# Attention's query products as three one-pass products of split operands, with keys and values for two batch elements at a time

## The chip, the cores and the metric

The kernel runs on one core of a Trainium2 chip. A core has a matrix engine (PE, whose weight loads are shown as PEld), a vector engine (DVE), a scalar engine (ACT), a general engine (POOL, also called GpSimd) and a queue for transfers (SP). Each engine takes its instructions in order and waits where an operand isn't there. PE writes its sums to PSUM, which has eight banks of 128 x 512 floats[...]. The metric is the time of one execution on the device, in microseconds, lower is better.

## The reference

The input x has 16 batch elements of 512 rows and 512 columns, the context 16 elements of 120 rows. The layer is cross attention with 16 heads of 32 columns and then a feed-forward layer with quantized weights and activations. In short:

```
xn   = layernorm(x)
q, k, v = xn @ Wq, ctx @ Wk, ctx @ Wv
q, k = rope(q), rope(k)
x1   = x + softmax(q k^T / sqrt(32)) v @ Wo
h    = act_qdq(layernorm(x1))        # scale: max |h| over all of x1
gate, up = act_qdq(h @ Wg^T), act_qdq(h @ Wu^T)
out  = x1 + act_qdq(act_qdq(gate * sigmoid_q(gate)) * up) @ Wd^T
```

`act_qdq` rounds to 16 bit with one scale for the whole tensor, so its scale is a maximum over everything before it. The weights of the feed-forward layer are rounded to 4 bit in blocks of 32.

## The kernel before

The kernel has three stages: attention (up to about 943 us), gate and up products, and the down product. Only attention and its hand-over are touched by the change.

In attention the loop `for b in range(B)` goes over the 16 elements, with a loop over four groups `g` of four heads inside. One iteration works on several elements at once: `here` (b) has its scores, exponentials and values computed; `nxt` (b + 1) has its queries projected and rotated; `new` (b + 2) is loaded, has row statistics, is normalized and turned so that its columns lie on partitions; `old` (b - 1) has its values divided by the sums, multiplied by Wo and added to x; `older` (b - 2) has its rows of x1 normalized and the maximum of |h| taken (`end_normalize`, `largest`). Beside this the keys and values of later elements are made by `Keys`, four elements at a time (`BC = 4`), in twelve parts that `go_on` hands out two or so per group, and in each of elements 1 to 12 a block of gate weights is quantized and split (`WeightBlock`).

The order on PE, DVE and ACT is the order in which the program is written (`manual_schedule`). POOL and the transfer queue are ordered by the planner of the framework. PSUM is divided into three single banks that everything takes in turn (`bank`, tag "w"), two pairs for the scores and one for the sums. So an operation that takes a bank waits until the third taker before it has been read.

Within a group the order is: `scores` (matmuls L338, then DVE takes maxima over rows, L344), some product of another element that fills PE, `maxima` (PE transposes the maxima, `tm`, L356, and DVE makes their negative, `nm`, L365), `values` of the group before, `exponentials` (PE subtracts the maxima, L373, ACT takes the exponential, L381). After that come the rest of the group's parts, such as outputs of `old` and, in group 3, the turning of `new`, the output of the last row block, and the turning of the gate weight.

The queries are exact float products: `query(g)` multiplies four blocks of 128 rows of the turned x (`xnT`, two buffers) with Wq (L317), and `rotate` applies the rotary tables with DVE and POOL. In the feed-forward stage the same accuracy is had otherwise: an operand is split into a high and a low part (`Pieces`: mix, lo, hi), and three products in a one-pass format are added, with one division of the bank by ACT between the first and the other two (`sums`, `MIXED`, `WHOLE`).

Of the kernel before, what the change touches and what calls it, by code (L numbers as in the profile page):

```python
# [21 lines left out]
P = 128  # L22
# [20 lines left out]
HI_BITS = -4096  # L43
TO_256 = 1.5 * 2.0 ** 31
# [9 lines left out]
def tile_xattn_ffn(  # L54
# [24 lines left out]
    BC = 4  # L79
# [14 lines left out]
    max_x = const.tile([P, B * NQ], F32, name="max_x")  # L94
# [93 lines left out]
    with ExitStack() as at:  # L188
# [18 lines left out]
        def transposed(src, rows, dst, nm):  # L207

            n = src.shape[1] // P
            tp = bank(f"tp_{nm}").rearrange("p (n r) -> p n r", r=P)  # L210
            for i in range(n):
                nc.tensor.transpose(tp[:, i, :rows], src[:, ts(i, P)], ident[:rows, :rows])
            nc.scalar.copy(dst, tp[:, :n, :rows])  # L213
# [18 lines left out]
        class Keys:  # L232


            def __init__(self, c):
# [5 lines left out]
                if c == 0:  # L241
# [4 lines left out]
                self.parts = [  # L246
                    (f, i) for f in (self.context, self.value, self.key) for i in range(BC)
                ]

            def go_on(self, n):  # L250
                for _ in range(n):
                    if self.parts:
                        f, i = self.parts.pop(0)
                        f(i)

            def context(self, i):
                if self.c == 0:
                    ct = self.ct[:, i, :]
                else:
                    ct = p1.tile([SK, D], F32, tag="ct", name=f"ct_{self.c}_{i}")  # L260
                    nc.sync.dma_start(ct, cx[self.c * BC + i])
                transposed(ct, SK, self.cT[:, :, ts(i, SK)], f"c_{self.c}_{i}")

            def value(self, i):
                ps = bank(f"vp_{self.c}_{i}")
# [5 lines left out]
                nc.scalar.copy(self.vt[:, i, :], ps[:SK])  # L271

            def key(self, g):
                ps = bank(f"kp_{self.c}_{g}")[:, :SKC]
# [6 lines left out]
                rotate(self.kT[:, g, :, :SK], ps, bc(cos_k), bc(sin_k), f"k_{self.c}_{g}")  # L281
                nc.gpsimd.tensor_copy(self.kT[:, g, :, SK:], self.kT[:, g, :, : P - SK])

        class Element:


            def __init__(self, b):
                self.b = b
                self.xt = p2.tile([P, NQ, D], F32, tag="xt", name=f"xt_{b}", bufs=4)
                nc.sync.dma_start(self.xt, x[b].rearrange("(q p) d -> p q d", p=P))  # L290
                self.mv = p2.tile([P, NQ, 2], F32, tag="mv", name=f"mv_{b}")
                self.rstd = p2.tile([P, NQ], F32, tag="rstd", name=f"rstd_{b}")
                self.xnT = p1.tile([P, ND, S], F32, tag="xnT", name=f"xnT_{b}")
                self.qs, self.xn = [], {}
# [6 lines left out]
            def normalize(self, q, engine=nc.gpsimd):  # L301
                xn = p2.tile([P, D], F32, tag="xn", name=f"xn_{self.b}_{q}", bufs=3)
# [6 lines left out]
            def turn(self, q):  # L309
                transposed(self.xn.pop(q), P, self.xnT[:, :, ts(q, P)], f"x_{self.b}_{q}")  # L310

            def query(self, g):

                nm = f"{self.b}_{g}"
                ps = bank(f"qp_{nm}")
                for d in range(ND):
                    nc.tensor.matmul(  # L317
                        ps, lhsT=wq_sb[:, d, ts(g, P)], rhs=self.xnT[:, d, :],
                        start=(d == 0), stop=(d == ND - 1),
                    )  # L320
                def rest():
                    qT = p1.tile([P, S], F32, tag="qT", name=f"qT_{nm}", bufs=5)
                    rotate(qT, ps, cos_q, sin_q, f"q_{nm}")
# [96 lines left out]
            def output(self, q):  # L420

                ps = bank(f"op_{self.b}_{q}")
# [5 lines left out]
                def rest():  # L428
                    b, x1 = self.b, self.xt[:, q, :]
                    nc.vector.tensor_tensor(x1, ps, x1, ALU.add)  # L430
                    row_stats(p2, x1, ln_mv[:, b, q, :], f"f_{b}_{q}")
                return rest
# [9 lines left out]

            def end_normalize(self, q, engine=nc.gpsimd):
                b = self.b
# [1089 lines left out]
```

## Time and profile before

Three runs took 2604.33 us in the median (2603.31 to 2606.76). The profiled execution took 2608.83 us, with a span of 2607.0 us.

| stage | us | PE busy | DVE busy | ACT busy | POOL busy | clock |
|---|---|---|---|---|---|---|
| start, 0 to 58 | 58 | 51.85 | 26.18 | 9.90 | 22.90 | 1.00 |
| elements 0 to 14, 58 to 862 | 804 | 776.27 | 633.14 | 210.25 | 487.14 | 0.99 |
| element 15, 862 to 911 | 49 | 39.17 | 31.96 | 12.68 | 10.31 | 0.90 |
| end of attention, 911 to 943 | 32 | 25.57 | 22.66 | 1.34 | 17.33 | 0.87 |
| feed-forward, 943 to 2607 | 1664 | 1619.80 | 1369.62 | 921.69 | 1038.97 | 0.99 |

"Busy" is the time in which the engine had an instruction under way. The clock is the share of full speed that TensorE was granted. The table says which engine is full in a stage; what a wait is worth has to be read from the timeline, since engines run in order and a wait of one delays all that stands behind it. In a timeline line the first number is the start in us from the span's start, the second the length; then engine, line, operation, the tile written and those read, the shape and how many instructions were merged. A note in brackets gives the idle time before it and what ended it.

### The profile page before, as it was taken

The page shows a single profiled execution, that of the slowest core. Times are in us where ns is not written, and L with a number is a line of the kernel's source. Part 1 is how long each engine was busy: PE and PEld are TensorE (multiplying, and loading weights), DVE is VectorE, ACT ScalarE, POOL GpSimd, SP SyncE. Part 2 cuts the span into 40 slices and gives each one's busy share as a digit, 9 for nine tenths or more (in the row PEclk, how much of TensorE's full clock was granted, in tenths as well). Part 3 has the DMA queues.
Part 4 walks back from the last instruction along what each step waited for, and adds up shares of the span by engine and source line. Part 5 has one row for each costly group of instructions (what it writes and reads, how often), then busy time and mean ns, then how long its engine had stood idle before and what let it go on. Part 6 is the DMA issues. An engine that isn't in the chain of part 4 may idle for free. (4 is left out here: it accounts for less than half of the span.)

```text
span 2607.0 us, 30411 instructions
## 1 busy us (share of the span) xinstructions
PE 2512.7 (96%) x10732; PEld 1690.9 (65%) x10732; DVE 2083.6 (80%) x2836; ACT 1155.9 (44%) x1311; POOL 1576.6 (60%) x1011
## 2 busy tenths in 40 slices
PE   8899999999999889999999999999999699999999
PEld 4334344333433268888878888888887478788887
DVE  4668886887888667786887589999998688888886
ACT  1222232222222225545445378888877344444442
POOL 3466665655675165545555057777766477777775
PEclk9899999999999989999999999999999799999999
DMA  4011121111120086767766789999889777777774
GB/s 161 20 65 49 49 93 59 57 59 49 49 77 33 22 277 214 250 202 244 226 217 217 238 300 332 322 344 330 296 290 322 295 280 253 248 248 248 251 249 145
DMA packets 268146, 500.49 MB, mean 192 GB/s; under 512 B 47440, under 2 KB 66000, under 8 KB 267984
## 3 DMA queue, kind: packets, MB, share of 16 engines
q1 hardware_dynamic: 267296, 496.90, 55.6%
q8 instruction: 85, 1.39, 0.2%
q10 hardware_dynamic: 528, 1.05, 0.1%
q14 instruction: 77, 0.63, 0.1%
q0 software_dynamic: 160, 0.52, 0.1%
HBM read 263.00 MB, written 227.54 MB: 188 GB/s over the span
## 5 line engine op out<-in xcount | busy, mean ns | idle before, releaser
L758 POOL TENSOR_SCALAR oh_d<-oq_d 128x512 fp32r<-128x512 int16 x190 | 398.0, 2117 | 160.8 <-DVE oq_d L1320 134.1
L1106 POOL TENSOR_TENSOR po<-gt,t_wu 128x1024 f32<-128x1024 f32 x96 | 231.7, 2413 | 208.2 <-DVE gt L1083 149.6
L317 PE MATMUL qp<-xnT,wq_sb 128*128 128x512 f32 x512 | 239.2, 610 | 2.5 <-ACT cT L213 2.5
L398 ACT COPY ao<-pv 128x512 f32<-128x512 f32 x64 | 37.5, 586 | 452.2 <-PE pv L389 452.2
L424 PE MATMUL op<-wo_sb,ao 128*128 128x512 f32 x512 | 233.2, 604 | 0.2 <-DVE ao L418 0.2
L1337 PE MATMUL dn_d<-wd,om_d 128*128 128x512 f32 x768 | 196.7, 406 | 22.7 <-DVE om_d L768 13.4
L782 PE MATMUL mm_wg<-xl_g,wg 128*128 128x512 f32 x768 | 205.4, 389 | 0.0
L782 PE MATMUL mm_wg<-xh_g,wg 128*128 128x512 f32 x768 | 205.4, 389 | 0.0
L868 PE MATMUL mm_wg<-xm_g,wg 128*128 128x512 f32 x768 | 195.7, 396 | 6.8 <-DVE xm_g L768 3.6
L1320 DVE SCALAR_TENSOR_TENSOR oq_d<-pq_d,r_o,uq_d 128x1024 int16<-128x1024 int16 x96 | 127.3, 1326 | 90.1 <-ACT uq_d L1273 90.1
L229 POOL TENSOR_TENSOR rt_q<-rt_q,sin_q 128x512 f32<-128x512 f32 x64 | 81.3, 1271 | 185.0 <-DVE rt_q L226 185.0
L1337 PEld LDWEIGHTS dn_d<-wd,om_d 128*128 128x128 f32 x768 | 145.9, 194 | 68.3 <-DVE om_d L768 31.0
L758 POOL TENSOR_SCALAR xh_g<-xq_g 128x512 fp32r<-128x512 int16 x60 | 117.5, 1982 | 116.6 <-DMA xq_g<-xi 111.2
L1337 PE MATMUL dn_d<-wd,ol_d 128*128 128x512 f32 x768 | 184.6, 389 | 1.0 <-ACT dn_d L1349 1.0
L1337 PE MATMUL dn_d<-wd,oh_d 128*128 128x512 f32 x768 | 184.5, 389 | 0.0
L782 PE MATMUL mm_wu<-xl_u,wu 128*128 128x512 f32 x672 | 180.5, 390 | 1.3 <-ACT mm_wu L874 1.3
L317 PEld LDWEIGHTS qp<-xnT,wq_sb 128*128 128x128 f32 x512 | 93.3, 192 | 134.9 <-issue 111.0
L782 PE MATMUL mm_wu<-xh_u,wu 128*128 128x512 f32 x672 | 179.7, 389 | 0.0
L344 DVE TRANSPOSE_TENSOR_REDUCE mt<-st 128x32 f32<-128x1024 f32 x128 | 151.6, 1222 | 30.2 <-PE st L338 30.1
L891 DVE TENSOR_REDUCE max_g<-t_wg 128x1 f32<-128x1024 f32 x96 | 116.5, 1214 | 72.4 <-ACT t_wg L886 72.4
L424 PEld LDWEIGHTS op<-wo_sb,ao 128*128 128x128 f32 x512 | 94.5, 192 | 116.9 <-issue 104.6
L868 PEld LDWEIGHTS mm_wg<-xm_g,wg 128*128 128x128 f32 x768 | 142.9, 190 | 38.9 <-DVE xm_g L768 6.3
(266 smaller groups left out, 5682.7 us busy)
## 6 DMA issues: line engine op xcount, KB each, us to landing
g_d<-t_wg SPq DMA_DIRECT2D x96, 512.0 KB, 3.7
gt<-g_d SPq DMA_DIRECT2D x96, 512.0 KB, 5.4
u_d<-t_wu SPq DMA_DIRECT2D x90, 512.0 KB, 5.8
p_d<-gt SPq DMA_DIRECT2D x90, 512.0 KB, 5.1
p<-p_d SPq DMA_DIRECT2D x90, 512.0 KB, 6.0
u<-u_d SPq DMA_DIRECT2D x90, 512.0 KB, 5.3
xt<-in_x_dram SPq DMA_DIRECT2D x16, 1024.0 KB, 5.3
x_d<-x SPq DMA_DIRECT2D x32, 512.0 KB, 5.0
```

Source lines behind the costliest of these rows:

```text
L229: nc.gpsimd.tensor_tensor(v(t), v(t), sin, ALU.mult)
L317: nc.tensor.matmul(ps, lhsT=wq_sb[:, d, ts(g, P)], rhs=self.xnT[:, d, :], start=(d == 0), stop=(d == ND - 1),)
L344: nc.vector.tensor_reduce(self.mt[:, 2 * i : 2 * i + 2, 0, :], self.st[i].rearrange("p h (c j) -> p h c j", j=DK), AX.X, ALU.max, apply_tr ...
L398: nc.scalar.copy(self.ao[:, g, :], pv)
L424: nc.tensor.matmul(ps, lhsT=self.ao[:, g, ts(q, P)], rhs=wo_sb[:, g, :], start=(g == 0), stop=(g == NG - 1),)
L758: engine.tensor_scalar(as_runs(p.hi, q), q, TO_256, TO_256, ALU.add, ALU.subtract)
L782: nc.tensor.matmul(ps[:, j, :], lhsT=lhs(j, i)[k], rhs=rhs(j, i)[k], start=(k == 0 and i == 0), stop=(k != 1 and i == n - 1), skip_group_c ...
L868: nc.tensor.matmul(self.ps[:, j, :], lhsT=lhs(j, d), rhs=self.x.p[d].mix, start=(d == 0), stop=(d == ND - 1), skip_group_check=True,)
L891: nc.vector.tensor_reduce(maxes[:, i : i + 1], self.t, AX.XYZ, ALU.max, **how)
L1106: nc.gpsimd.tensor_tensor(flat(g.po), flat(g.tile), flat(c.t), ALU.mult)
L1320: nc.vector.scalar_tensor_tensor(out=oq.rearrange("p f t -> p (f t)"), in0=pq, scalar=r_o, in1=uq, op0=ALU.mult, op1=ALU.mult,)
L1337: nc.tensor.matmul(self.ps[j], lhsT=self.p[f // 2].all()[k][:, f % 2, ts(j, P)], rhs=wd.made[f][k], start=(k == 0 and f == 0), stop=(k != ...
```

## The change

- **Queries.** The turned block of x is no longer kept as one exact tile. `turn(q)` writes it back over the normalized rows and masks its high bits (DVE) to `up`, of which there are two buffers. `halve(q)` copies these to `hi` (ACT) and subtracts them from the full value for `lo` (POOL). `mixed(q)` multiplies `lo` by -4096 (ACT) and adds `hi` for `mix` (POOL). The three pieces have one buffer each. Wq is split in the same way before the loop (`query_weight`).
- **Query sums.** `query(g)` makes the first four one-pass products (mix) and ACT divides the bank; `query_rest(g)` makes the other eight (lo, hi) and returns the rotation. Eight instructions become twelve. The factor that makes up for the division goes into the rotary tables.
- **Keys and values.** `BC` is 2; there are eight batches with eight parts each, four parts per element, and key products have 240 columns instead of 480.
- **x1.** The rows of x are loaded again for the output (`load("xr")`), with three buffers instead of four. The sum `x1` is made by an instruction that also gives each row's maximum, and DVE takes the row's minimum. `end_normalize` and `largest` go; at the end the maxima and minima are normalized (two operations on 128 x 128 values), and the largest magnitude is taken from them.
- **Order.** Fillers between `scores` and `maxima` are put in two lists: `soon` runs before `maxima`, `late` after it. The first passes of queries 0 and 1 come after the exponentials of group 0 where keys are made.

The diff, cut to its core:

```diff
-    BC = 4
+    BC = 2
...
-                self.xt = p2.tile([P, NQ, D], F32, tag="xt", name=f"xt_{b}", bufs=4)
-                nc.sync.dma_start(self.xt, x[b].rearrange("(q p) d -> p q d", p=P))
+                self.load("xt")
...
+            def load(self, nm):
+                self.xt = p2.tile([P, NQ, D], F32, tag="xt", name=f"{nm}_{self.b}", bufs=3)
+                nc.sync.dma_start(self.xt, x[self.b].rearrange("(q p) d -> p q d", p=P))
...
             def turn(self, q):
-                transposed(self.xn.pop(q), P, self.xnT[:, :, ts(q, P)], f"x_{self.b}_{q}")
+                if q == 0:
+                    self.mix, self.lo, self.hi = self.pieces = [
+                        p1.tile([P, ND, S], F32R, tag=f"xn{k}", name=f"xn{k}_{self.b}", bufs=1)
+                        for k in "mlh"
+                    ]
+                full = self.xn[q].rearrange("p (d r) -> p d r", r=P)
+                transposed(self.xn[q], P, full, bank(f"tp_{self.b}_{q}"))()
+                self.up[q] = p2.tile([P, ND, P], F32, tag="xu", name=f"xu_{self.b}_{q}")
+                nc.vector.tensor_scalar(
+                    self.up[q].bitcast(I32), full.bitcast(I32), HI_BITS, None, ALU.bitwise_and
+                )
+
+            def halve(self, q):
+                m, l, h = (t[:, :, ts(q, P)] for t in self.pieces)
+                full = self.xn.pop(q).rearrange("p (d r) -> p d r", r=P)
+                nc.scalar.copy(h, self.up[q])
+                nc.gpsimd.tensor_tensor(l, full, h.bitcast(F32), ALU.subtract)
+
+            def mixed(self, q):
+                m, l, h = (t[:, :, ts(q, P)] for t in self.pieces)
+                low = self.up.pop(q)
+                nc.scalar.mul(low, l.bitcast(F32), -SPLIT)
+                nc.gpsimd.tensor_tensor(m, low, h.bitcast(F32), ALU.add)
+
+            def query_sums(self, g, ks):
+                for k in ks:
+                    for d in range(ND):
+                        nc.tensor.matmul(
+                            self.qp[g], lhsT=wq_pieces[k][:, d, ts(g, P)],
+                            rhs=self.pieces[k][:, d, :], start=(k == 0 and d == 0),
+                            stop=(k != 1 and d == ND - 1), skip_group_check=True,
+                        )
 
             def query(self, g):
...
+                self.qp[g] = bank(f"qp_{self.b}_{g}")
+                self.query_sums(g, (0,))
+                nc.scalar.mul(self.qp[g], self.qp[g], MIXED)
+
+            def query_rest(self, g):
+                self.query_sums(g, (1, 2))
                 def rest():
...
-                    nc.vector.tensor_tensor(x1, ps, x1, ALU.add)
+                def add():
+                    nc.vector.tensor_tensor_reduce(
+                        out=x1, in0=ps, in1=x1, scale=1.0, scalar=-LARGEST, op0=ALU.add,
+                        op1=ALU.max, accum_out=ends_x[:, b, q, 0:1],
+                    )
+                def stats():
                     row_stats(p2, x1, ln_mv[:, b, q, :], f"f_{b}_{q}")
+                    nc.vector.tensor_reduce(ends_x[:, b, q, 1:2], x1, AX.X, ALU.min)
+                return add, stats
...
+            if old:
+                old.load("xr")
+            if nxt:
+                nxt.halve(NQ - 1)
+                nxt.mixed(NQ - 2)
+                nxt.mixed(NQ - 1)
+            here.attend()
             for g in range(NG):
+                here.scores(g, keys[b // BC].kT)
+                soon, late = [], []
                 if g == 0:
+                    if kvs:
+                        kvs.go_on()()
+                        late.append(kvs.go_on())
+                    elif nxt:
+                        nxt.query(0)
+                        nxt.query(1)
+                        late.append(nxt.query_rest(0))
+                if g == 1:
+                    first_bank = bank("kv") if kvs else None
+                    if nxt:
+                        nxt.query(2)
+                    if kvs:
+                        soon.append(kvs.go_on(first_bank))
+                    if nxt:
+                        late.append(nxt.query_rest(2))
+                if g == 2:
+                    first_bank = bank("op") if old else None
+                    if nxt:
+                        nxt.query(3)
+                    if old:
+                        add, stats = old.output(0, first_bank)
+                        soon.append(add)
+                        late.append(stats)
+                    if nxt:
+                        late.append(nxt.query_rest(3))
+                if g == 3 and old:
+                    late += old.output(2)
+                for f in soon:
+                    f()
                 here.maxima(g)
...
                 if g == 0:
+                    if nxt and kvs:
+                        nxt.query(0)
+                        nxt.query(1)
                     if old:
                         old.reciprocals()
+                    if nxt and kvs:
+                        nxt.query_rest(0)()
                     if nxt:
-                        nxt.query(1)()
+                        nxt.query_rest(1)()
...
                 if g == 3:
                     if new:
                         new.turn(0)
-                        new.normalize(3)
                     if old:
-                        old.output(3)()
+                        for f in old.output(3):
+                            f()
                         old.end()
                         old.inverse()
                     if new:
                         new.turn(1)
+                        new.halve(0)
                     if weight:
                         rest = weight.turn(0)
                     if new:
+                        new.mixed(0)
                         new.turn(2)
+                        new.halve(1)
+                        new.mixed(1)
                         new.turn(3)
+                        new.halve(2)
                     if weight:
                         rest()
```

## The prediction

> **What bounds the kernel now.** I read the page's engine table and 40 slices first. The attention stage is the left third: there PE is 9 or 8 in nearly every slice while DVE is at 4 to 8. The chain of waits that ended last holds only lines of the feed-forward stage, so it says nothing about this change. I therefore cut the attention stage into its elements. Element b begins with its first score matmuls (L338): b = 4 at 277.9 us, b = 6 at 377.1, b = 7 at 438.1. Columns are length, then busy time of PE, PEld, DVE, ACT, POOL, then clock.
>
> ```profile
> 277.90:326.50 48.60, 47.10 (x205) 18.70 (x204) 43.69 (x79) 13.46 (x19) 31.99 (x30) 1.00 0.20 65
> ...
> 377.10:438.10 61.00, 60.33 (x237) 24.48 (x236) 43.04 (x79) 15.85 (x23) 32.02 (x30) 1.00 0.15 53
> 438.10:498.40 60.30, 59.63 (x237) 24.71 (x236) 47.72 (x91) 13.48 (x19) 42.36 (x42) 1.00 0.15 53
> ```
>
> PE leaves 0.7 to 1.5 us of an element idle, so PE sets the pace and its clock is full. Yet in element 4 DVE has 43.7 us of work in 48.6. Elements 6 and 7 carry the value and key products of a batch of four. Elements 1 to 12 take 664.3 us (103.4 to 767.7), 55.4 each.
>
> **What the query products save.** Within one element the queries are four groups of eight exact-float matmuls (two instructions per product). Their weight loads start 0.43 us apart (439.71, 440.14, 440.57), so a group holds PE for 8 x 0.43 = 3.43 us.
>
> ```profile
> L317 PE MATMUL qp<-xnT,wq_sb 128*128 128x512 f32 x384 | 177.6, 605 | 2.5 <-ACT cT L213 2.5
> ...
> L229 POOL TENSOR_TENSOR rt_q<-rt_q,sin_q 128x512 f32<-128x512 f32 x49 | 62.3, 1271 | 139.7 <-DVE rt_q L226 139.7
> ```
>
> The feed-forward stage already runs one-pass products of the same shape. From its timeline:
>
> ```profile
> 1105.64 1.07 PE L782 MATMUL mm_wg<-xl_g,wg 128*128 128x512 f32 x4
> 1106.55 1.07 PE L782 MATMUL mm_wg<-xh_g,wg 128*128 128x512 f32 x4
> ```
>
> Four start every 0.907 us: 0.227 each, 12 x 0.227 = 2.72 us a group. The saving is 0.71 us a group, 2.85 an element, 64 x 0.71 = 45 us in all, if PE stays the bound.
>
> **What it adds, per element.** For each of four row blocks (128x512): a DVE mask (`up`), an ACT copy (`hi`), a POOL subtraction (`lo`), an ACT product and a POOL sum (`mix`). POOL takes 1.27 us for each (the row above), so 8 x 1.27 = 10.2 us, against four removed normalizations of 2.08 = 8.3. POOL has room. ACT adds 8 x 0.63 (its product from SBUF, L176) and 4 x 0.59 for dividing the query banks: 7.4 us on 13 to 16 busy. DVE swaps four maxima of 0.67 for four minima of 0.67. The mask is not in the trace from SBUF; nearest is the table scaling at 17.63, 0.42 us, so 4 x 0.45. The add that also yields a maximum has no near row: between 0 and 0.2 us over the 0.68 of L430, I take 0.1. DVE gains about 2 us. The reload of x is 1 MB per element: loads of this size land in 5.3 us, it is issued some 25 us before use, and DMA is 15% busy, so nothing; uncovered it would cost 5 us. Keys for two instead of four: half the columns in twice as many groups, so the same PE sum. The step cannot fall below the 0.19 us weight load; I take 0.22 against 0.20 for half of the 0.40 step, under 1 us an element, which I put at nothing beside the waits below.
>
> **Where it waits.** This decides. PE, DVE and ACT run in the written order. Around the change of element the trace shows this (T0 = 432.14, when the first block of the element after next is turned):
>
> ```profile
> 432.14 0.66 PE L212 MATMUL tp_x<-ident,xn 128*128 128x128 f32 x4
> ...
> 434.12 0.59 ACT L213 COPY xnT<-tp_x 128x512 f32<-128x512 f32 x1
> ...
> 438.10 1.14 PE L338 MATMUL st<-qT,kT 32*128 32x512 f32 x8
> ...
> 438.59 0.69 DVE L175 TENSOR_TENSOR wt_wg<-tp_wg,wt_wg 128x512 f32<-128x512 f32 x1
> ...
> 439.28 2.38 DVE L344 TRANSPOSE_TENSOR_REDUCE mt<-st 128x32 f32<-128x1024 f32 x2
> ...
> 442.71 0.27 PE L356 MATMUL tm<-ident,mt 128*128 128x128 f32 x1
> ```
>
> The score maxima on DVE begin at T0+7.1 and PE's transposition of them (`tm`) is at T0+10.6; a query group (3.43) fills PE between. In the new order DVE has the four masks and the weight block's two operations ahead of those maxima. There are two `xu` buffers, so the third mask waits for block 0's sum, the fourth for block 1's. ACT is in order too: block 0's product stands ahead of the copy of block 2, block 1's ahead of block 3's. The chain, with about 0.1 us a hand-over: weight quantization ends T0+4.7 (0.8 later than today, by one minimum); mask 0 5.2; hi 5.9; lo 7.3; product 8.0; sum 9.4; lo of block 1 10.7 (POOL is taken till 9.4); product 11.4; sum 12.8; mask 3 13.4; weight operations 14.75; maxima 17.35; `tm` T0+17.6. That is **7 us later**, and ahead of it PE has only two context transpositions (0.9, even elements) or two key groups (3.5, odd ones).
>
> Behind `tm`: in even elements ACT's context copy stands behind block 3's product (18.9), and the bank of pv waits for it, so the exponentials leave PE at 21.9. Both query passes now come after that (4 x 0.91 + 4 x 0.45 = 5.4 us, where one group of 3.43 stood), and the second pass waits for ACT: two exponentials (1.94) and the division (0.6), some 1.3 us idle. The next scores start at T0+28.4 in even elements, T0+27.4 in odd ones. Today they start at T0+23.1 (455.27) with two wide key groups of 6.45; with the new key or context work and no saving on the queries that would be 17.5 and 20.2. Loss: 10.9 and 7.2.
>
> In group 2 the second query pass stands ahead of `tm`, so DVE idles early and is late with the next element's statistics. The second output product waits for a bank until query 3 is rotated, at 12.4 us after the group's scores instead of 9.9. I work out T0 of the next element at 23.6 us after group 2's scores, today 21.5: 2.1 lost. Group 1 comes out level in even elements and 0.7 shorter in odd ones. **Net: even +13.0, odd +8.6.** Over elements 1 to 12: 6 x 13.0 + 6 x 8.6 = +130.
>
> **Two rules weighed against rows.** DVE's scalar operations slow beside POOL:
>
> ```profile
> 43.70 1.11 DVE L303 TENSOR_SCALAR xn<-xt,mv,rstd 128x512 f32<-128x512 f32 x1
> ...
> 44.61 1.26 POOL L230 TENSOR_TENSOR kT<-ra_k,rt_k 128x480 f32<-128x480 f32 x1
> ```
>
> The same shape takes 0.52 alone (936.80). By this row one exposed mask costs 0.6 more: 12 x 0.6 = 7 us. The Trainium skill, SBUF — State Buffer, Who interferes with whom, says the shared port pair is locked for a whole instruction, so the mask could wait out 1.27 us: 15 us. I take 7.
>
> The clock: after 3.1 us of idle PE in the last element, the same eight pv matmuls (1.06 at 442.92) read
>
> ```profile
> 866.63 1.94 PE L389 MATMUL pv<-e,vt 120*32 120x512 f32 x8
> ```
>
> The Trainium skill, TensorE: Matmul & The Clock Gate, Why this matters for your kernels, says to allow no idle gap over about 3 us, as one idle window returns the array to half rate. My chain has a gap of 4 to 6 us in every element. By the row pv and the sums cost 1.6 more, 12 x 1.6 = 19 us; by the rule's window of 3.4 us at half rate up to 40. Part runs while PE waits for ACT anyway; I take 0 and keep 40 for the range.
>
> **Ends.** Start: splitting Wq and element 0 puts 16 POOL operations (20 us) after 21 us, so the first query starts near 48 against 42.25, while halved keys, values and query groups give time back: +4. Element 0: +7 (it takes half a batch's keys and the late `tm`). Element 13: +12, 7 of it key work moved there. Element 14: +6, its first query waits for block 3's sum. Tail: the last normalization and maximum before the scale go, -2. Sum +27.
>
> 130 + 7 + 27 = **+164 us** on the span of 2607: 2771. The execution itself took 2608.8, 4.5 above the median of the runs, 2604.3; on their scale **2766**.
>
> **Rivals.** (1) The saving arrives: the masks do not hold DVE and the second pass finds its bank divided. Then 2604 - 45 + 3 = 2562. For it: PE is full today and ACT and POOL are not. Against: the written order. It decides where the maxima begin before about T0+8.5, one POOL-ACT round earlier than each of two I count. (2) Part hidden: only the late `tm` is paid, one round instead of two, about +5 an element: 12 x 5 and half of the ends, near 2680. (3) Half clock in every element plus full port waits: 2766 + 40 + 8 = 2814. (4) Saving and waits cancel: no change.
>
> **How the numbers follow.** Worked chain, with (3) as its upper part: 0.60, own range 2690 to 2830. Part hidden: 0.22. No change: 0.03. Faster: 0.15. A measurement here tells about 0.2% (5 us) from nothing. So slower 0.82, same 0.03, faster 0.15. The range 2612 to 2832 leaves out the faster case and little above.
>
> **What would show it.** L317's successor at 0.227 us a step; in elements 2 to 12 the first `tm` some 17 us after the first turned block; PE busy under 85% of those elements; DVE idle ahead of masks until POOL's sums; element length 64 to 69 us; clock under 1.00. It is wrong if PE stays above 95% busy there, or if elements come out under 55 us.

## The result and the profile after

The changed kernel takes **2817.3 us** in the median of its runs (2815.7 to 2818.9), against 2603.8 for the kernel before on the same chip: a ratio of 1.0819, with a 95% interval of 1.0801 to 1.0838. It is 8.2% slower. The forecast was 2766, in a range of 2612 to 2832: the direction and the mechanism were right, and of a loss of 213 us I had counted 162.

The span of the profiled execution is 2817.1 us, 210 longer than before. The 16th element's first scores start at 1080.0 us instead of 862.0, so the attention stage has lost 218, and what follows it has gained 8. Here are the rows of PE and of its granted clock from the page's 40 slices, each digit a tenth, of the kernel before and then of the changed one:

```profile
PE   8899999999999889999999999999999699999999
PEclk9899999999999989999999999999999799999999
```

```profile
PE   5678787878787878899999999999999879999999
PEclk8889898989898999999999999999999989999999
```

Attention was the first 14 or 15 slices and is now the first 16 or so. PE was at 8 or 9 there; from the third slice on it now alternates between 7 and 8, and the clock is no longer full. The same cut into elements as before (element 5, then element 6: length, then busy time of PE, PEld, DVE, ACT, POOL, then clock):

```profile
400.77:466.58 65.81, 55.85 (x253) 29.23 (x252) 51.76 (x99) 20.01 (x30) 40.35 (x46) 0.90 0.18 64
466.58:539.97 73.39, 54.65 (x246) 25.80 (x245) 47.72 (x87) 22.17 (x34) 33.69 (x34) 0.88 0.19 65
```

No engine is full any more. In element 6, PE has 54.65 us of work in 73.39 and DVE 47.72. So the time is in waits, and a sum of busy times cannot show it. Elements 1 to 12 take 830.0 us, 69.2 each, where they took 55.4. They lie at 72.7 to 73.9 for even numbers, above the 64 to 69 forecast, and mostly at 65.1 to 65.8 for odd ones.

The wait is in the first group. It takes 28.5 to 29.7 us in even elements and 24.6 to 25.2 in odd ones (21.6 in element 1); before it was 10.7 to 17.6. This is the timeline of the changed kernel from element 5 to element 6 (start, length, engine, line, operation; in brackets the idle time before it and what ended it). T0, where the first block is turned, is 460.10:

```profile
460.10 0.66 PE L213 MATMUL tp<-ident,xn 128*128 128x128 f32 x4
...
464.42 0.42 DVE L324 TENSOR_SCALAR xu<-xn 128x512 int32<-128x512 int32 x1
...
465.96 1.26 POOL L332 TENSOR_TENSOR xnl<-xn,xnh 128x512 fp32r<-128x512 f32 x1 [2.33 <-issue]
...
467.68 1.04 POOL L123 TENSOR_TENSOR r_f<-ve_f,mhalf 128x4 f32<-128x4 f32 x1
...
469.79 1.26 POOL L338 TENSOR_TENSOR xnm<-xu,xnh 128x512 fp32r<-128x512 f32 x1
471.01 1.26 POOL L332 TENSOR_TENSOR xnl<-xn,xnh 128x512 fp32r<-128x512 f32 x1
471.08 1.47 DVE L324 TENSOR_SCALAR xu<-xn 128x512 int32<-128x512 int32 x1 [3.58 <-POOL xnm L338]
...
474.31 1.47 DVE L324 TENSOR_SCALAR xu<-xn 128x512 int32<-128x512 int32 x1 [1.76 <-POOL xnm L338]
475.70 0.68 DVE L175 TENSOR_SCALAR wt_wg<-tp_wg 128x512 int32<-128x512 int32 x1
476.41 0.69 DVE L176 TENSOR_TENSOR wt_wg<-tp_wg,wt_wg 128x512 f32<-128x512 f32 x1
477.02 2.37 DVE L384 TRANSPOSE_TENSOR_REDUCE mt<-st 128x32 f32<-128x1024 f32 x2
...
479.43 0.95 DVE L389 COPY mt<-mt 128x64 f32<-128x64 f32 x1
479.57 0.88 SPq L583 DMA_DIRECT2D wg_d<-wt_wg  x2
...
480.50 5.06 SPq L260 DMA_DIRECT2D ct<-in_ctx_dram  x2
...
484.15 1.03 PE L213 MATMUL kv<-ident,ct 120*128 120x120 f32 x4 [15.10 <-DMA ct<-in_ctx_dram]
484.97 0.42 PE L396 MATMUL tm<-ident,mt 128*128 128x128 f32 x1
485.32 1.94 PE L429 MATMUL pv<-e,vt 120*32 120x512 f32 x8
...
494.77 1.07 PE L343 MATMUL qp<-xnh,wq_h 128*128 128x512 f32 x4
495.77 1.14 PE L378 MATMUL st<-qT,kT 32*128 32x512 f32 x8
```

Read it from the top. The third and the fourth mask (L324) each wait for a sum of pieces on POOL (L338), because the sum reads the buffer they write. Behind them on DVE stand the weight block's two operations, and behind those the score maxima (L384). What PE has to do next stands behind the turning of these maxima (`tm`, L396), which comes 24.9 us after T0; before the change that was 10.6. In even elements one more thing holds it: the second context of a batch. Its load stands in SP's queue behind the stores of the weight block and is waited for on PE ahead of `tm`. The next scores start at T0+35.7. The product steps themselves are as forecast: four one-pass products start within 0.9 to 1.0 us.

What PE waited for between 188 and 956 us says the same as a list (waiting instruction, what it waited for; total us, number of waits, longest):

```profile
PE kv L213 <- DMA ct<-in_ctx_dram: 90.3, 6, 15.3
PE tm L396 <- DVE mt L389: 37.2, 16, 4.7
```

This list must be read with care. The first row puts 15 us of each even element on a transfer. DVE's copy of the maxima ended at 480.38, so had the transfer been there, PE would still have waited until then: 4.6 us of the 15 belong to the transfer, and the rest to the chain above it.

### The profile page after: what moved, and what is told of

The parts are those of the page before. It is cut to its first block, busy times and chain, and to the rows that moved or that the text cites. A ratio compares the mean times of both kernels' runs of the same rounds, so it can differ in the third digit from the quotient of the medians.

```text
span 2817.1 us, 31863 instructions
## 1 busy us (share of the span) xinstructions
PE 2515.3 (89%) x11116; PEld 1771.3 (63%) x11116; DVE 2161.7 (77%) x3014; ACT 1265.5 (45%) x1511; POOL 1633.3 (58%) x1135
## 3 DMA queue, kind: packets, MB, share of 16 engines
q10 hardware_dynamic: 528, 1.05, 0.1%
## 5 line engine op out<-in xcount | busy, mean ns | idle before, releaser
L962 PE MATMUL mm_wu<-xm_u,wu 128*128 128x512 f32 x672 | 166.4, 390 | 0.2
L1443 ACT ACTIVATE dn_d<-dn_d 128x512 f32<-128x512 f32 x64 | 37.2, 582 | 286.0 <-PE dn_d L1431 283.4
L1431 PEld LDWEIGHTS dn_d<-wd,ol_d 128*128 128x128 f32 x768 | 144.1, 188 | 31.3 <-ACT dn_d L1443 1.4
```

The costliest lines, as they stand in the source:

```text
L962: nc.tensor.matmul(self.ps[:, j, :], lhsT=lhs(j, d), rhs=self.x.p[d].mix, start=(d == 0), stop=(d == ND - 1), skip_group_check=True,)
L1431: nc.tensor.matmul(self.ps[j], lhsT=self.p[f // 2].all()[k][:, f % 2, ts(j, P)], rhs=wd.made[f][k], start=(k == 0 and f == 0), stop=(k != ...
```

## The experiments

My theory: the loss is the chain of rounds between DVE, ACT and POOL that splits the turned blocks, with DVE's written order behind it. The rivals: the transfer of the context, the clock of PE, the port that DVE and POOL share, or the keys for two elements at a time. Most runs take out one of them. In the diffs the changed kernel is the start unless another is named.

**Two buffers for the context.** (The exponentials get two buffers instead of four, to make room in SBUF, the memory of the core beside PSUM. This is so in all runs below that build on it.)

```diff
-    name=f"ct_{self.c}_{i}", bufs=1)
+    name=f"ct_{self.c}_{i}", bufs=2)
```

> The changed kernel with two context buffers instead of one (room from the exponentials' tiles, two instead of four). Theory 1, the context load is a wait of its own: in even elements the first tm comes at about T0+20.6, when DVE has the maxima, instead of T0+24.9; 4.3 us in seven elements, near 2787 us. Theory 2, the load lies in the gap that the masks make and the next wait takes its place: under 5 us, 2812 or more.

Measured: 2798.5 us (2795.6 to 2805.6), 19 less. The even elements' first group goes from 29 to 25.5 us, the odd ones stay at 25.2. The wait list for PE between 188 and 956 us now reads

```profile
PE tm L396 <- DVE mt L389: 78.5, 23, 5.9
```

and no row names the context's transfer. So the transfer was on the path, but for 3.3 to 3.9 us in every second element, not for 15. What remains is the chain.

**The split left out.** Two buffers for the context, and elements 2 to 15 take their queries from element 1's pieces: no masks, high copies, subtractions, products or sums for them.

```diff
             def turn(self, q):
+                if self.b > 1:
+                    self.pieces = el[1].pieces
+                    full = self.xn.pop(q).rearrange("p (d r) -> p d r", r=P)
+                    transposed(full.rearrange("p d r -> p (d r)"), P, full, bank(f"tp_{self.b}_{q}"))()
+                    return
...
             def halve(self, q):
+                if self.b > 1:
+                    return
...
             def mixed(self, q):
+                if self.b > 1:
+                    return
```

> The changed kernel with two context buffers, and with the splitting of elements 2 to 15 left out (their masks, copies to hi, subtractions, products and sums; their queries are made from element 1's pieces; turns and all matmuls stay). Theory 1, the chain of the split is the loss: g0 falls from 25 us to 13 to 15, elements to 55 to 58, near 2650 us; what is then left over the kernel before is the order of the query passes and of groups 2 and 3. Theory 2, the three passes with their division, or the keys for two, cost as much: 2720 or more.

Measured: 2642.9 us (2640.4 to 2648.6). Against the 2798.5 of the run above, the split's operations and their waits are worth 156 us. Elements 6 and 7, cut as before:

```profile
408.74:465.97 57.23, 52.32 (x246) 25.29 (x245) 43.25 (x83) 17.72 (x27) 23.82 (x26) 1.00 0.25 83
465.97:520.24 54.27, 51.09 (x254) 27.53 (x253) 46.44 (x95) 15.63 (x23) 30.23 (x38) 1.00 0.23 77
```

The clock is full and the first group is down to 13.4 to 15.0 us in elements 2 to 13. So the split is the main loss; its 156 us include the clock that comes back when its waits go. The run also shows a second thing: even without the split, with one-pass queries, elements 1 to 12 take 56.3 us each, and not less than the 55.4 of the kernel before. PE is idle for 4.9 and 3.2 us of the two shown, so the saving on the queries does not come through. The keys for two elements do not explain that: the kernel before with these alone (a run below) needs 676.2 us for elements 1 to 12 with exact queries, and this one 676.1.

**Another order of the same work.** Four buffers `xu`, and all turns and masks run first; products and sums come in the next iteration.

```diff
+    name=f"xu_{self.b}_{q}", bufs=4)
...
                     if new:
-                        new.mixed(0)
                         new.turn(2)
-                        new.halve(1)
-                        new.mixed(1)
                         new.turn(3)
+                        new.halve(1)
                         new.halve(2)
...
                 nxt.halve(NQ - 1)
-                nxt.mixed(NQ - 2)
-                nxt.mixed(NQ - 1)
+                for q in range(NQ if b else 2):
+                    nxt.mixed(q if b else q + 2)
```

> The changed kernel with four mask buffers and with ACT's four products (and POOL's sums) behind all turns, masks and copies, so that no mask and no copy stands behind a POOL round trip; same work. Theory 1, the round trips POOL-ACT hold DVE: the first maxima begin near T0+10.5 instead of T0+16.9, elements get 5 to 6 us shorter although the last sum, due near T0+18.6, now holds query 0; near 2740 us. Theory 2, the half clock or the sum of DVE's work sets the length: under 15 us, 2800 or more.

Measured: 2759.9 us (2756.3 to 2763.8), 57 less than the changed kernel. The masks no longer wait for a sum.

**Both together.** The order above with two buffers for the context.

> Both at once: the new order and two context buffers. Theory 1: the gains add up, even elements 9 us shorter and odd ones 6, near 2715 us. Theory 2, one wait hides behind the other: no lower than the better of the two by over 5 us.

Measured: 2753.2 us (2752.1 to 2754.5). The two gains do not add: 57 and 19 give 64. The timeline of this kernel shows what is late next:

```profile
379.30 1.31 DVE L324 TENSOR_SCALAR xu<-xn 128x512 int32<-128x512 int32 x3
...
385.18 0.33 PE L396 MATMUL tm<-ident,mt 128*128 128x128 f32 x1 [1.59 <-DVE mt L389]
...
386.38 1.20 DVE L536 SCALAR_TENSOR_TENSOR mh<-mh,low_m,mx 128x32 fp32r<-128x32 f32 x1
387.50 4.17 POOL L338 TENSOR_TENSOR xnm<-xu,xnh 128x512 fp32r<-128x512 f32 x3
...
387.62 1.70 DVE L405 TENSOR_TENSOR nm<-mh,nrow 128x512 fp32r<-128x512 f32 x1
...
392.27 1.27 POOL L338 TENSOR_TENSOR xnm<-xu,xnh 128x512 fp32r<-128x512 f32 x1
...
393.59 0.79 PE L343 MATMUL qp<-xnm,wq_m 128*128 128x512 f32 x1 [3.42 <-POOL xnm L338]
```

Three masks now take 1.31 us together. `tm` comes 12.7 us after this element's T0 (372.52), where the kernel before had it at 10.6. But the sums are put off, and the query product waits for the last of them. Since POOL's sums now run beside DVE's work on the maxima, that work is stretched as well (0.25 to 1.20 and 0.69 to 1.70 us).

**The split a group earlier.** With two buffers for the context and four `xu`, statistics and normalization of the new element come at the end of group 1, the turns at the end of group 2 and the start of group 3. The products follow group 3's exponentials, and query 0 stands ahead of the maxima.

```diff
+                if g == 3 and new:
+                    new.turn(2)
+                    new.turn(3)
+                    new.halve(1)
...
-                if new and g == 2:
-                    for q in range(NQ):
-                        new.stats(q)
-                    for q in range(NQ):
-                        new.normalize(q)
...
+                if g == 1 and new:
+                    for q in range(NQ):
+                        new.stats(q)
+                    for q in range(NQ):
+                        new.normalize(q)
+                if g == 2 and new:
+                    new.turn(0)
```

> The changed kernel rearranged: statistics and normalization of the element after next at the end of group 1, its turns at the end of group 2 and the start of group 3, copies to hi and products spread behind the exponentials of group 3; query 0 in front of the first maxima again; four mask buffers, two context buffers. Same work. Theory 1, only the place of the split costs: the first tm is at most 1 us later than in the kernel before, elements 53 to 55 us, start some 8 us longer, 2585 to 2615 us in all. Theory 2, DVE has too much work and POOL's port holds it: elements 57 us or more, above 2640.

Measured: 2762.4 us (2759.2 to 2766.5): no better than the other order, and a clear miss. In its timeline:

```profile
380.64 2.94 POOL L332 TENSOR_TENSOR xnl<-xn,xnh 128x512 fp32r<-128x512 f32 x2 [5.39 <-ACT xnh L331]
380.65 1.81 DVE L154 TENSOR_TENSOR wq_wg<-wt_wg,wr_wg 128x512 int16<-128x512 f32 x1
...
382.50 1.23 DVE L157 TENSOR_SCALAR wq_wg<-wq_wg 128x512 int16<-128x512 int16 x1
...
383.77 1.63 DVE L158 TENSOR_TENSOR wt_wg<-wq_wg,ws_wg 128x512 f32<-128x512 int16 x1
...
385.50 0.85 PE L166 MATMUL tp_wg<-ident,wt_wg 128*128 128x128 f32 x4 [3.84 <-issue]
...
388.88 0.63 ACT L177 ACTIVATE wt_wg<-wt_wg 128x512 f32<-128x512 f32 x1 [6.75 <-DVE wt_wg L176]
...
393.34 2.07 PE L343 MATMUL qp<-xnm,wq_m 128*128 128x512 f32 x4 [4.97 <-POOL xnm L338]
```

The subtractions now fall on the quantization of the weight block (1.81 us instead of 0.69, 1.23 instead of 0.35), and the sums on its last step (1.63 instead of 0.69). PE idles 3.84 us and turns that weight block (L166) 0.1 us after this step has ended; the bracket names no releaser, but the turn reads what the step writes. ACT's product for blocks 2 and 3 stands behind its operation for that weight block (L177), for which it idles 6.75 us. So the last sum is late again, and the query product waits for it as in the run before. The wait was moved, not removed.

**The clock.** Products on constants fill PE's gaps, so that its clock stays up: 56 ahead of the second context's transposition in even elements, 12 ahead of a key product and 10 ahead of `tm` in odd ones.

```diff
+        def busy(ps, n):
+            for _ in range(n):
+                nc.tensor.matmul(
+                    ps, lhsT=ones, rhs=rep.rearrange("p g m -> p (g m)"), start=True, stop=True
+                )
...
+                if self.c and i:
+                    busy(ps, 56)
...
+                if self.c and g == 1:
+                    busy(ps, 12)
...
+                if g == 0 and self.b % BC:
+                    busy(tp, 10)
```

> The changed kernel with idle one-pass products put into PE's gaps of group 0 (56 ahead of the second context's transpositions in even elements, 12 ahead of the second key product and 10 ahead of tm in odd ones), so that PE isn't idle before tm. Theory 1, half rate after the gap is on the path: pv, sm and the first query passes run at full rate, 2 to 3 us less in each of 14 elements, near 2785 us, and the granted clock rises from 0.951. Theory 2, PE waits for ACT there in any case: within 6 us of 2817.

Measured: 2833.3 us (2825.5 to 2837.7), which neither theory expected. The whole is therefore undecided, but its parts can be read. An even element (T0 = 468.36):

```profile
481.73 15.85 PE L218 MATMUL kv<-rep,ones 128*128 128x512 f32 x56 [4.42 <-ACT xn L214]
...
497.82 0.27 PE L409 MATMUL tm<-ident,mt 128*128 128x128 f32 x1
498.02 1.07 PE L442 MATMUL pv<-e,vt 120*32 120x512 f32 x8
...
506.77 1.14 PE L388 MATMUL st<-qT,kT 32*128 32x512 f32 x8
```

In the changed kernel the granted clock was 0.50 from `tm` (484.97) to 488.90. Here the eight products `pv` take 1.07 us instead of 1.94, and from `tm` to the next scores it is 8.95 us instead of 10.80 (484.97 to 495.77). The gain lies in `pv` and the sums behind it, where PE waits for nobody; over the six even elements it is 1.8 us in the mean. In odd elements the same stretch shrinks from 11.38 to 9.96, but this is an upper bound: `tm` itself comes up to 1.4 us later there (T0+21.7 instead of 20.3), so that DVE has less left to do behind it, and the next scores start at T0+31.7 as before. So the half clock costs 1.8 us on the path of an even element and at most 1.4 of an odd one, 11 to 19 us over twelve. The added products started late, ran past the transfer they were to fill in for, and put `tm` at T0+29.5 instead of 24.9: that ate the gain.

**Keys and values for two elements, alone, in the kernel before.**

```diff
-    BC = 4
+    BC = 2
...
-            if b % BC == 1 and b // BC + 1 < B // BC:
+            if b % BC == 0 and b // BC + 1 < B // BC:
```

(and four key parts for each batch still).

> The kernel before with one part of the change alone: keys and values for two elements at a time. Theory 1, same work in other places: 2598 to 2610 us. Theory 2, key products of 240 columns run into their weight loads and the rotations' fixed parts double: 2615 or more.

Measured: 2623.4 us (2620.9 to 2626.7), ratio 1.0065 (1.0051 to 1.0079): it costs 17 us by itself. Elements 6 and 7 of this kernel:

```profile
376.87:433.03 56.16, 54.32 (x230) 22.44 (x229) 43.50 (x79) 15.58 (x23) 32.00 (x30) 1.00 0.19 66
433.03:488.70 55.67, 53.27 (x237) 24.68 (x237) 45.58 (x91) 13.48 (x19) 38.20 (x42) 1.00 0.17 57
```

PE idles 1.8 and 2.4 us here, where the elements shown of the kernel before left 0.7 to 1.5. Elements 1 to 12 take 676.2 us against 664.3, and element 13 takes 7.1 more, but element 1 begins 10.8 earlier. So the last element's first scores are 8.1 us late; the rest of the difference lies behind them, where both kernels have the same work, and was not explained.

**x1's maxima and minima alone, in the kernel before.** The rows are kept as they were, without a second load; `end_normalize` and `largest` go.

```diff
-                    nc.vector.tensor_tensor(x1, ps, x1, ALU.add)
+                    nc.vector.tensor_tensor_reduce(
+                        out=x1, in0=ps, in1=x1, scale=1.0, scalar=-LARGEST, op0=ALU.add,
+                        op1=ALU.max, accum_out=ends_x[:, b, q, 0:1],
+                    )
                     row_stats(p2, x1, ln_mv[:, b, q, :], f"f_{b}_{q}")
+                    nc.vector.tensor_reduce(ends_x[:, b, q, 1:2], x1, AX.X, ALU.min)
...
-                    if older:
-                        for q in range(3):
-                            older.end_normalize(q)
```

> The kernel before with one part of the change alone: maxima of x1's rows by the add and minima by DVE, no end_normalize and largest (x is not reloaded, four buffers as before). Theory 1, this part costs nothing and shortens the tail: 2600 to 2604 us. Theory 2, the add with accumulator and the minimum make DVE late in groups 2 and 3: 2610 to 2620.

Measured: **2592.7 us** (2587.7 to 2595.1, seven runs) against 2606.0, ratio 0.9955 (0.9938 to 0.9972). This part gains 13 us, more than expected, and the version beats both kernels. Elements 6 and 8 of it:

```profile
368.63:429.82 61.19, 60.54 (x238) 24.45 (x237) 42.60 (x83) 15.84 (x23) 23.86 (x26) 1.00 0.15 52
490.37:538.20 47.83, 47.08 (x206) 18.66 (x205) 42.33 (x83) 13.49 (x19) 23.86 (x26) 1.00 0.19 67
```

In element 8 POOL has 23.9 us instead of the 32.0 of element 4 before, and DVE 42.3 instead of 43.7, while PE is full. The first scores of element 15 are 12.0 us earlier (850.0 against 862.0). Of that 3.1 lies ahead of element 2 and 3.3 in it. Most of the rest is 0.8 to 1.2 in each element without value and key products, such as element 8: PE's idle time there is 0.75 us, and was 1.5 in the like element 4. Which of the removed operations frees it was not tested.

**The masks out of PSUM.** Three runs go on from the two buffers for the context (2798.5), and take the chain apart. In the first the mask reads the bank in which PE left the turned block, not its copy in SBUF.

```diff
-                transposed(self.xn[q], P, full, bank(f"tp_{self.b}_{q}"))()
+                ps = bank(f"tp_{self.b}_{q}")
+                transposed(self.xn[q], P, full, ps)()
...
-                    self.up[q].bitcast(I32), full.bitcast(I32), HI_BITS, None, ALU.bitwise_and
+                    self.up[q].bitcast(I32), ps.rearrange("p (d r) -> p d r", r=P).bitcast(I32),
+                    HI_BITS, None, ALU.bitwise_and
```

> The changed kernel with two buffers for the context (as in the earlier run, 2798.5 us), and the mask of a turned block reads the PSUM bank in which TensorE left it, not the copy in SBUF. Theory 1: a mask in SBUF that meets a subtraction of GpSimd waits for the shared port (1.47 us instead of 0.42, two of them in a row on the path). A mask out of PSUM takes some 0.7 us whatever GpSimd does, so 14 elements gain 2 x 0.8 = 1.6 us: 22 us, 2776. Theory 2: the masks are off the path, since VectorE waits for GpSimd's sums later anyhow: within 6 us of 2798.

Measured: 2784.2 us (2783.2 to 2784.3), 14 less. In the timeline:

```profile
527.33 1.27 POOL L334 TENSOR_TENSOR xnl<-xn,xnh 128x512 fp32r<-128x512 f32 x1
527.41 0.69 DVE L325 TENSOR_SCALAR xu<-tp 128x512 int32<-128x512 int32 x1 [3.23 <-POOL xnm L340]
```

The mask starts 0.08 us after POOL's subtraction, as in the changed kernel, but takes 0.69 us instead of 1.47. So the stretch is on the path, and that it goes when the source is in PSUM fits the shared port on the SBUF side. The size was forecast too high: elements 2 to 12 are 0.7 to 1.3 us shorter, 1.1 in the mean, not 1.6. Only the fourth mask's stretch is paid: it starts at T0+14.2 in both kernels, since it waits for POOL's sum, and ends 0.8 us earlier here.

**The inverse deviations.** POOL works out the inverse deviations of the old element (L122 to L127) between the first subtraction and the first sum. First the call was moved a group later.

```diff
                         old.end()
-                        old.inverse()
...
+                if g == 1 and b > 1:
+                    el[b - 2].inverse()
```

> The changed kernel with two buffers for the context (2798.5 us), and the inverse deviations of an old element, which GpSimd works out ahead of the first sum of pieces (2.5 us), moved to the next element's second group. Theory 1: GpSimd's chain of subtractions and sums is what VectorE's last masks and the maxima wait for, so each of 14 elements gains 1.6 to 2.5 us: 22 to 35 us, 2764 to 2776. Theory 2: GpSimd's chain moves ahead and its operations now meet the masks of other blocks, the path stays: within 6 us of 2798.

Measured: 2798.5 us (2792.3 to 2799.6), as if nothing had been changed. Nothing had been: the trace of this kernel has POOL in the old order, since the planner orders POOL.

```profile
527.51 1.27 POOL L332 TENSOR_TENSOR xnl<-xn,xnh 128x512 fp32r<-128x512 f32 x1 [2.34 <-issue]
528.87 0.28 POOL L122 TENSOR_SCALAR ve_f<-ln_mv 128x4 f32<-128x4 f32 x1
529.23 1.04 POOL L123 TENSOR_TENSOR r_f<-ve_f,mhalf 128x4 f32<-128x4 f32 x1
```

The run decides nothing about the wait. With this edit and the masks out of PSUM together:

> Both edits at once. If both theories 1 hold and the waits stand one behind the other on the path: 2798.5 - 22 - 28 = 2748. If one wait hides behind the other: no better than the better of the two alone by more than 6 us.

Measured: 2782.8 us (2781.0 to 2785.7). That is the effect of the masks, and for the same reason it says nothing about the sum of both.

So the inverse was taken away in another manner: elements 1 to 13 have theirs worked out in one go, which cannot start before the last of their statistics.

```diff
                         old.end()
-                        old.inverse()
+                        if b in (1, B - 1):
+                            old.inverse()
+                        if b == B - 2:
+                            flat = lambda t: t.rearrange("p b q -> p (b q)")
+                            inverse_std(
+                                p2, flat(ln_mv[:, 1 : B - 2, :, 1]), flat(ln_rstd[:, 1 : B - 2, :]),
+                                "f_1", bufs=1,
+                            )
```

> The changed kernel with two buffers for the context (2798.5 us), and the inverse deviations of elements 1 to 13 worked out once, in six operations behind the last of them, instead of at each element: the move before this one (inv) left them in the trace where they were, ahead of the first sum, because the planner put them back, so it decided nothing. Theory 1: the 2.5 us of GpSimd ahead of the first sum of pieces are on the path, through the third and fourth mask, which wait for sums to free their buffers: of the wait of 3.6 us ahead of the third mask about 2 us go, 12 elements x 1.7 to 2.3 = 20 to 28 us, 2770 to 2778. Theory 2: the subtraction of block 1, which stands in the same place, or ScalarE's products are late next, and less than 0.5 us an element is gained: 2792 to 2800.

Measured: 2777.1 us (2774.5 to 2777.2), 21 less. POOL in the trace:

```profile
520.23 1.27 POOL L332 TENSOR_TENSOR xnl<-xn,xnh 128x512 fp32r<-128x512 f32 x1 [2.34 <-issue]
522.24 1.27 POOL L338 TENSOR_TENSOR xnm<-xu,xnh 128x512 fp32r<-128x512 f32 x1 [0.74 <-ACT xu L337]
```

The sum now starts 2.0 us after the subtraction, where it was 3.8; what it waits for is ACT's product. Elements 3 to 12 are 1.4 to 2.4 us shorter, 1.8 in the mean. So small operations that the planner fitted into a hole of POOL lay on the path.

## Why the prediction was right, and where its sizes were off

- **What bounds the kernel, and what the queries save.** Right: PE was full before, and a step of the one-pass products takes 0.227 us. PE has the saving as work; in the run without the split it does not arrive as time, since PE waits there too. That run takes as long in elements 1 to 12 as the one with exact queries and the keys for two alone (676.1 and 676.2), so the keys do not account for it. What does, the place of the query passes or the work in groups 2 and 3, was not separated.
- **The chain from T0.** Right in mechanism: masks wait for sums, the maxima stand behind the masks, `tm` behind the maxima, and the run without the split puts 156 us on it. Its times ran late. The first mask ended at T0+4.7, a little ahead of the 5.2 forecast. The first sum ended at T0+11.0 instead of 9.4, because the planner put the inverse deviations ahead of it: I had counted POOL's work as room and had not asked what the planner would place in the hole. One run shows 21 us for this. The fourth mask ended at 15.7 instead of 13.4, and the maxima with their copy at 20.3 instead of 17.35.
- **The port.** I chose the row (0.6 a mask, 7 us) over the rule of the Trainium skill (SBUF — State Buffer, Who interferes with whom), by which the port is locked for a whole instruction (15 us). The rule was nearer: a mask beside POOL takes 1.05 us more than alone, and the run with masks out of PSUM gains 14. I had also read the row wrongly. The operation of 1.11 us at 43.70 did not meet the POOL operation that I set beside it (44.61) but the one before:

```profile
43.33 1.20 POOL L229 TENSOR_TENSOR rt_k<-rt_k,sin_k 128x480 f32<-128x480 f32 x1 [0.47 <-DVE rt_k L226]
```

It began 0.37 us into this one and lasted until 0.28 us after its end, as the masks do. A mask that starts just behind the start of POOL's operation of 1.26 us then takes 1.47, so row and rule say the same. Not counted at all: the copy of the maxima, 0.95 us instead of 0.20.

- **The clock.** I put it at nothing and kept 40 for the range. It is 11 to 19 us; the row of the last element had given 1.6 an element, 19, and I had it in hand. The 40 was a wrong sum besides: it takes the rule's window of 3.4 us as lost, but at half rate only half of it is lost, 1.7 us an element and 20 in all (an estimate from the figure of the Trainium skill, TensorE: Matmul & The Clock Gate, that the prediction used). So here too row and rule agree.
- **Transfers.** The reload of x costs nothing visible, as forecast. The context load is the term that is missing from the sum. With two elements a batch, its second context is needed in the first group of even elements, with a single buffer, and its load is issued on SP behind the stores of the weight block. I had looked at the new transfer and not at the one whose deadline had moved. It put `tm` of even elements 4.6 us later, and two buffers bring back 19 us.
- **Even and odd.** Forecast with the port: +13.6 and +9.2; measured +17.9 and +9.7 over the mean of 55.4. The even ones, which have the context load, make nearly all of the difference in elements 1 to 12: 166 us instead of 137.
- **Keys for two.** Put at nothing; alone they cost 17 us. The sum of PE's work is what I said (108 us for elements 6 and 7 in that run, and as much on average before; the step of 240 columns is 0.203 us, less than the 0.22 I took), but PE has about 1 us more of idle time an element.
- **Group 2.** Forecast 2.1 us lost up to the next T0; measured 22.4 us from scores to T0 in group 2 and its successor against 21.5 before, so 0.9.
- **Ends.** Forecast +27, measured +44: start +8.6 instead of 4, element 0 +14.3 instead of 7, element 13 +16.1 instead of 12, element 14 +13.3 instead of 6, tail -7.9 instead of -2 (of which up to 4.5 may be that the profiled execution of the kernel before lay that much above its median). I had worked these with one delay each, but they have the same chain as the others. The part with x1's maxima, which I costed at 2 us of tail, gains 13 alone.
- **The rivals.** The third (half clock in every element and full waits for the port, 2814) came out nearest to 2817, but not by its own reasons alone: the clock is at most half of what it gave, and the inverse deviations, the context load and the ends make up for it. The terms that I had left out, each as measured by itself (19 context, 21 inverse, 11 to 19 clock, 7 more for the port), add to 58 to 66, more than the 29 that are missing in elements 1 to 12. The traces show where the rest went. From T0 to the second group's scores even elements take 35.6 us in the mean and odd ones 31.5 (without element 1), where I had 28.4 and 27.4: some 68 us more over twelve elements, 61 without the 7 counted for the port. Some 37 came back: group 1 takes 15.3 and 11.7 us against 17.1 and 14.2 in the kernel with the keys for two alone (I had it level, and 0.7 shorter), and group 2 loses 0.9 instead of 2.1. So the delay up to the second group was over half as large again as forecast (18.1 and 11.3 us instead of 10.9 and 7.2), and the total came as near as it did partly by luck, since these errors have opposite signs. The first rival (the saving arrives) needed the maxima to begin before T0+8.5; they begin at T0+16.9.

What stays open: whether any order makes the split free. Two were tried. Products and sums put off bring back 57 us of the 213, and 64 with two buffers for the context; the split a group earlier, with both sets of buffers, brings back 55 and runs into the weight block's work on DVE and ACT. No order that spreads the split over a whole element was tried.

## What to carry to other kernels

When a change takes work from the full engine and gives a little to three idle ones, draw the added operations as a chain with its hand-overs, at the place in each engine's order where they stand: here 45 us of saved PE work, which no run shows as saved time, bought a chain that costs 156. Two buffers for an operand that DVE writes, ACT overwrites and POOL reads make each block wait for the whole round of the one two before it. Look for what else may be placed in the holes (a planner's small operations, a queue's earlier stores), and price a wait of the full engine with the clock it comes back at.

## What the hardware showed that I had not expected

- Some DVE operations that start beside a two-operand operation of POOL last until 0.05 to 0.6 us after POOL's end: the mask 1.47 us instead of 0.42, the copy of the maxima 0.95 instead of 0.20, a small multiply-add 1.20 instead of 0.25. Others do not: the row statistics (L113) take 0.69 and the row minimum (L478) 0.65 us in either case. The same mask reading PSUM takes 0.69 beside POOL and alone. So SBUF is the faster source when POOL is idle, and PSUM when it is not.
- The add that also yields each row's maximum is two instructions in the trace, 0.68 to 0.69 and 0.08 us. That is the 0.1 over the plain add that I had taken between its bounds.
